# A two-layer graph attention network on one core: another order of work for the last four superchunks of a layer, and one cast moved in the prologue

## The chip, the cores and the metric

The kernel runs on one core of one Trainium2 chip. The core has engines with queues of their own that run side by side: PE multiplies matrices (its weight loads are listed as PEld), DVE and ACT do elementwise work, POOL issues the gathers here (indirect DMAs), and SP issues the other transfers. Each engine takes its own instructions strictly in program order, and waits for the others by semaphores. The metric is the device time of one execution in microseconds (us); lower is better.

## The reference, cut to what matters

There are N = 6250 nodes with 256 features and E = 200000 edges, sorted by destination. The input goes through a layer norm and a ReLU, then through two graph attention layers (4 heads of 64, then 1 head of 256), and is added back at the end.

```python
def _gat(x, src, dst, ea, Wg, a_s, a_d, Wge, a_e, b, n, h, f):
    hx = (x @ Wg).reshape(n, h, f)
    he = (ea @ Wge).reshape(-1, h, f)
    al = leaky_relu(einsum('nhf,hf->nh', hx, a_s)[src] + einsum('nhf,hf->nh', hx, a_d)[dst]
                    + einsum('ehf,hf->eh', he, a_e), 0.2)
    m = segment_max(al, dst, num_segments=n)
    al = exp(al - m[dst])
    al = al / segment_sum(al, dst, num_segments=n)[dst]
    out = segment_sum(hx[src] * al[:, :, None], dst, num_segments=n)
    return out.reshape(n, h * f) + b

te = relu(edge_attr @ We0 + be0) * exp(x @ Wo0 + bo0)[src][:, None]
s2, d2, ea2 = _add_self_loops(src, dst, te, n)      # a loop per node, its features the mean of its edges
x = relu(_gat(x, s2, d2, ea2, Wg0, as0, ad0, Wge0, ae0, bg0, n, HEADS, PH) + x)
te = relu(edge_attr @ We1 + be1) * exp(x @ Wo1 + bo1)[src][:, None]
s2, d2, ea2 = _add_self_loops(src, dst, te, n)
x = _gat(x, s2, d2, ea2, Wg1, as1, ad1, Wge1, ae1, bg1, n, 1, D) + x
return x + orig
```

## The kernel before

**Tiling.** The edges lie in 1563 chunks of 128 (an edge to a partition). A superchunk is 24 chunks (C), and a layer has NS = 66 of them, numbered s = 0 to 65; the last two have 14 and 13 chunks. One pass of the main loop is one superchunk, called a step: k = 0 to 131, layer 0 first (k = 66 is s = 0 of layer 1). The destinations of a superchunk fit into 128 nodes, so its sums are matrix products with one-hot rows S (onehots, L945): each chunk adds S^T G to an accumulator u in PSUM (sums, L1120, two matmuls a chunk). The table T holds a row per node (T[0] of layer 0 is built in the prologue, T[1] of layer 1 is stored by layer 0's steps as their nodes are finished), and G is the rows gathered from it for the edges' sources.

**A step.** With st the step in hand, nx the next, pv the one before and pf the one before that, a step consists of these parts. The names are the functions of the kernel:

- gather(nx), L817: POOL issues an indirect DMA for each chunk of the next step, into one of three G buffers (step k uses buffer k mod 3, so it waits for the sums of step k - 3).
- rphase1(nx), L901 and L906: edge features of the next step, PE into y (one PSUM buffer), ACT into R (one buffer), twice each. load_ea(k + 2), L842, then loads edge features for the step after it (for two steps at a time, one buffer).
- logits(st), L1002 to L1017: DVE; waits for G. ends(st), L1025: PE transposes the scanned maxima into lf.
- spread(nx) and parts(nx), L930, L931, L955 to L960: DVE and one matmul into zad.
- sums(pv): the sums of the step before, on PE.
- links(st), L1035 and L1037 on DVE, then a transpose on PE into lf, L1042.
- blocks(nx), L967, onehots(st), L945 (S has two buffers), finish(pf), L1144 to L1209 in layer 0 and L1149 to L1237 in layer 1: DVE, nodes of the step before last.
- evict(pv) and carry(pv), L1125, L1131, L1133: ACT copies u to U, PE and ACT take out the row that goes on into the next superchunk. carried (L1092 to L1100) adds this row to G of the step in hand, ahead of its sums.
- rows1, rows2, rows3 of pf (L1215 and L1217; L385; L389, L1227): in layer 0 the new table row, by PE, ACT and DVE; rows3 ends with the store to T[1] on SP's queue (L1256). In layer 1 rows3 stores the output: by SP (L1261), or for the last two steps by POOL (L1264, L1265).
- rphase2(nx) and adst(nx), L915 and L974: PE, into zad.
- maxima(st), L1052 to L1079: DVE, waits for the link transpose in lf; ACT makes the exponentials. scale(st), L1110: DVE, multiplies G by them.
- edge_rows(nx), L988 and L991: DVE, waits for adst(nx).

The order of all this is written out by hand. Steps with s = 63 and s = 64, and k = 0, are "at once": their sums, finish, rows, evict and carry run within the step itself. The last step of a layer has a function of its own, last.

**Between the layers.** last issues gather(66), the first of layer 1, with indices (src1) in which nodes of the last two superchunks point at a row of zeros. This gather therefore waits for the T[1] store of s = 63 only; the rows of 64 and 65 are added to G afterwards by matmul (turned_onehots makes the one-hots from a loaded v, L686 and L795; added, L785 and L788). gather(67) waits for the stores of 64 and 65 too, and those wait until gather(66) has landed.

**Prologue.** Tables are built by tiles of x while generators interleave other preparation; indices is one of them: it loads small integer tiles (sc0, bcol, drow, r4, src, dpv) by SP's queue and turns them into floats on DVE (L410 casts dpv to before, L412 casts sc0 to scf).

Of the kernel before, what the change touches and what calls it, by code (L numbers as in the profile page):

```python
# [22 lines left out]
F32 = mybir.dt.float32  # L23
# [8 lines left out]
P = 128  # L32
C = 24
# [45 lines left out]
class Kernel:  # L79
# [311 lines left out]
    def indices(self, wp):  # L391


        nc, cp, a = self.nc, self.cp, self.a
        NS, NCH, N = self.NS, self.NCH, self.N
        V = nc.vector
# [9 lines left out]
        dpv = wp.tile([P, NS], I32, name="dpv", bufs=1)  # L406
        nc.sync.dma_start(dpv, a["dpv"])
        yield
        self.before = cp.tile([P, NS], F32, name="before")
        V.tensor_copy(self.before, dpv)  # L410
# [77 lines left out]
        V.tensor_reduce(self.bad[0:1, 0:1], chk.rearrange("p a b -> p (a b)"), axis=AX.X, op=OP.add)  # L488
        yield
# [81 lines left out]
    def edges(self, ctx):  # L571
        nc = self.nc
# [33 lines left out]
        pv = pf = None  # L606
        ahead, rest = 1, None
        for k, st in enumerate(steps):
            nx = steps[k + 1] if k + 1 < len(steps) else None
# [4 lines left out]
            left = self.groups[ahead][0] - 2 - k if ahead < len(self.groups) else 99  # L614
            if rest is None and left <= 2:
                gi = self.index_load(ahead, self.xp)
                rest = self.index_group(ahead, self.xp, gi)
            if st["s"] + 1 == self.NS:
                self.last(st, pv, nx)
                pv = None  # L620
                continue
# [30 lines left out]
            at_once = k == 0 or self.NS - 3 <= st["s"]  # L652
            if at_once:
                self.sums(st)
# [3 lines left out]
            if rest is not None:  # L658
                for _ in range(7):
                    next(rest, None)  # L660
                if left <= 0:
                    drain(rest)
                    ahead, rest = ahead + 1, None
            pf, pv = pv, st

            if at_once:
                if pf:
                    drain(self.finish(pf))
                    self.rows1(pf)
                    self.rows2(pf)  # L670
                    self.rows3(pf)
                pf = None
                self.evict(st)
                self.carry(st)
            if k == 0 and self.early:
                self.redirect()
        self.flag()

    def last(self, st, pv, nx):

        nc = self.nc
# [5 lines left out]
        if pv and "U" not in pv:  # L687
            self.sums(pv)
            self.evict(pv)
            self.carry(pv)  # L690
        now, half = (C, C) if st["L"].l else (0, C // 2)
        self.onehots(st, 0, now)
        drain(self.logits(st))
        self.ends(st)
        self.onehots(st, now, half)
        self.links(st)
        self.load_fl(st["k"] + 1)
        self.onehots(st, half)
        y = self.rphase1(nx) if nx else iter(())
        next(y, None)  # L700
        next(y, None)
# [3 lines left out]
        drain(y)  # L705
        self.load_ea(st["k"] + 2)
# [6 lines left out]
        if pv:  # L713
            if early:
                w0 = self.turned_onehots(nx, v, 0)
            self.rows1(pv)
            self.rows2(pv)
            self.rows3(pv)
        drain(self.finish(st))
# [394 lines left out]
    def sums(self, st):  # L1114
        nc, L, c = self.nc, st["L"], st["C"]
        G, S = st["G"], st["S"]
        st["u"] = u = self.ps_1.tile([P, 512], F32, name="u")
        for j in range(c):
            i = (j + 1) % c
            nc.tensor.matmul(u[:, :L.W], S[:, i, :], G[:, i, 0:L.W], start=(j == 0), stop=(j == c - 1))  # L1120
# [266 lines left out]
def drain(g):  # L1387
    for _ in g:
        pass
# [93 lines left out]
```

## Time and profile before

| what | us |
|---|---|
| median of 3 runs | 4138.07 (4133.18 to 4142.69) |
| the profiled execution, its time | 4140.48 |
| the profiled execution, its span in the profile | 4138.4 |
| POOL's first gather starts | 97.38 |
| gather(66), the first of layer 1, starts | 2113.58 |
| gather(67) starts | 2153.50 |
| POOL's last gather starts | 4083.89 |
| logits of k = 129, 130, 131 start | 4052.95, 4080.72, 4107.07 |
| scale of k = 129, 130, 131 starts | 4069.70, 4097.16, 4114.03 |
| the last U is evicted from | 4123.60 to 4123.99 |

The profile shows one execution. Its page has the busy time of each engine, the chain of waits that ended last, and the groups of instructions by line. The timeline lists single instructions: start, duration, engine, line, operation, output and inputs, how often, and in square brackets the idle time of the engine before it and what ended that ("[4.88 <-PE lf L1042]": 4.88 us idle, ended by PE's write of lf at L1042). SPq is the issue of a transfer on SP's queue. The clock in the tables of windows is the share of full speed that TensorE was granted.

### The profile page before, as it was taken

Reading aid. Unit: us, or ns where it says so; the run is one execution under the profiler, and the core shown is the slowest. Engines: PE = TensorE matmul, PEld = TensorE weight load, DVE = VectorE, ACT = ScalarE, POOL = GpSimd, SP = SyncE. Lnnn points to the kernel's source line nnn. Section 1 sums busy time; section 2 is a strip of 40 time slices with the busy share of each in tenths; the row PEclk is TensorE's granted clock in tenths of the full one; section 3 lists DMA queues with packets and bytes.
Section 4 is the critical chain, followed back from the end, with each engine's and each line's share of the span. In section 5 each row is a group of like instructions: output and inputs, shape, how many; then the busy total and the mean of one; then the engine's idle time right before and its main releaser. Section 6 shows DMA issues by size and latency. Waiting matters only on the chain.

```text
span 4138.4 us, 34955 instructions
## 1 busy us (share of the span) xinstructions
PE 2815.1 (68%) x10144; PEld 1863.5 (45%) x10144; DVE 2872.6 (69%) x6572; ACT 545.2 (13%) x1256; POOL 2988.4 (72%) x3158
## 2 busy tenths in 40 slices
PE   7577777777676776777676666656566666756665
PEld 5344444444454444544454444434344444434344
DVE  7587777777877778778766666666666666666665
ACT  5111111111111111111111010100101010010100
POOL 2777777777777777777647777777777777777773
PEclk9677877778787787777877777878777777777777
DMA  6545555555554555555435455445545554554552
GB/s 203 155 135 153 149 142 147 147 146 143 154 149 137 154 147 141 149 149 149 125 102 151 132 143 141 137 137 144 141 133 141 141 137 137 145 141 133 141 139 61
DMA packets 246794, 584.74 MB, mean 141 GB/s; under 512 B 63161, under 2 KB 103639, under 8 KB 246529
## 3 DMA queue, kind: packets, MB, share of 16 engines
q0 software_dynamic: 150144, 422.82, 38.7%
q1 hardware_dynamic: 96035, 158.96, 12.3%
q8 instruction: 81, 1.33, 0.1%
q14 instruction: 118, 0.97, 0.1%
q10 hardware_dynamic: 416, 0.67, 0.1%
HBM read 547.98 MB, written 34.34 MB: 141 GB/s over the span
## 4 chain that ended last, share of the span: by engine, by line
POOL 35%; PE 27%; DVE 19%; issue 14%; DMA 2%; ACT 2%; DVEq 0%; ACTq 0%; SPq 0%; POOLq 0%
POOL G L817 35%; PE u L1120 21%; DVE G L1110 9%; PE y L901 3%; DVE lb L930 1%; DMA G<-T,src 1%; PE fin L1131 1%; DVE rt L988 1%; ACT R L906 1%; PE fin L1215 1%; DVE G L1099 1%; ACT carry L1133 1%; DVE G L1079 0%; DVE t1row L389 0%; DVE crow L1095 0%
## 5 line engine op out<-in xcount | busy, mean ns | idle before, releaser
L817 POOL DMA_INDIRECT G<-T,src x3114 | 2970.0, 954 | 1092.2 <-issue 996.5
L1120 PE MATMUL u<-G,S 128*128 128x270 f32 (+1 forms) x6252 | 1714.1, 442 | 34.9 <-DVE G L1110 34.9
L1120 PEld LDWEIGHTS u<-G,S 128*128 128x128 f32 x6252 | 1370.1, 222 | 386.8 <-issue 41.1
L1110 DVE TENSOR_TENSOR G<-G,kps 128x6144 f32<-128x6144 f32 (+2 forms) x140 | 853.3, 6100 | 0.0
L901 PE MATMUL y<-ea,webd 64*128 64x384 f32 (+1 forms) x1056 | 512.4, 615 | 457.4 <-ACT R L906 455.3
L901 PEld LDWEIGHTS y<-ea,webd 64*128 64x128 f32 x1056 | 214.3, 224 | 677.8 <-ACT R L906 535.7
L945 DVE TENSOR_TENSOR S<-kps,loc 128x3072 f32<-128x3072 f32 (+2 forms) x133 | 436.4, 3281 | 0.0
L1025 PE MATMUL lf<-ident,fb 128*36 128x128 f32 (+1 forms) x132 | 54.0, 409 | 533.8 <-DVE fb L1017 306.3
L1025 PEld LDWEIGHTS lf<-ident,fb 128*36 128x36 f32 (+1 forms) x132 | 15.8, 119 | 651.6 <-DVE fb L1017 363.3
L906 ACT ACTIVATE R<-y,webd 128x768 f32<-128x768 f32 x260 | 231.9, 892 | 566.4 <-PE y L901 566.2
L1056 DVE SCALAR_TENSOR_TENSOR m<-fpen,lf,m 128x24 f32<-128x24 bf16 (+1 forms) x66 | 16.5, 250 | 378.9 <-PE lf L1042 378.6
L1002 DVE TENSOR_TENSOR G<-rt,G 128x96 f32<-128x96 f32 (+1 forms) x132 | 30.2, 229 | 262.8 <-DMA G<-T,src 256.7
L915 PE MATMUL zad<-R,wea 128*64 128x384 f32 (+1 forms) x1056 | 205.4, 510 | 0.3 <-DVE aq L967 0.3
L1059 DVE TENSOR_TENSOR mt<-fpen,lf 128x96 f32<-128x96 bf16 (+1 forms) x66 | 16.7, 253 | 253.8 <-PE lf L1042 253.8
L1125 ACT ACTIVATE U<-u 128x270 f32<-128x270 f32 (+1 forms) x132 | 51.8, 392 | 815.8 <-PE u L1120 815.8
L960 PE MATMUL zad<-a,Q 128*128 128x12 bf16 (+1 forms) x132 | 23.7, 179 | 169.3 <-DVE a L958 169.3
L1158 ACT ACTIVATE mw<-mw,mg 128x2 f32<-128x2 f32 x66 | 19.7, 298 | 885.7 <-DVE mg L1157 885.7
L988 DVE STREAM_TRANSPOSE rt<-zad 128x768 f32<-128x768 f32 (+1 forms) x130 | 124.4, 957 | 11.6 <-PE zad L974 11.6
L930 DVE TENSOR_TENSOR lb<-lb,kps 128x1536 bf16<-128x1536 bf16 (+1 forms) x68 | 113.0, 1662 | 12.8 <-DMA lb<-locrow 12.8
L915 PEld LDWEIGHTS zad<-R,wea 128*64 128x64 f32 x1056 | 66.2, 139 | 92.5 <-issue 58.8
L1131 PE MATMUL fin<-U,lsel 128*1 128x270 f32 (+1 forms) x260 | 79.1, 385 | 41.5 <-ACT U L1125 22.5
L1035 DVE TENSOR_TENSOR_SCAN cl<-fl,cl,lf 4x129 f32<-4x129 f32 (+1 forms) x130 | 60.7, 467 | 56.3 <-PE zad L960 52.9
(213 smaller groups left out, 2269.9 us busy)
## 6 DMA issues: line engine op xcount, KB each, us to landing
G<-T,src POOLq DMA_INDIRECT x3114, 2.8
ea<-in_ea_dram SPq DMA_DIRECT2D x64, 768.0 KB
lb<-locrow SPq DMA_DIRECT2D x64, 384.0 KB
T<-t1row SPq DMA_DIRECT2D x66, 260.0 KB
tw<-T SPq DMA_DIRECT2D x66, 258.0 KB
tw<-T SPq DMA_DIRECT2D x66, 134.0 KB
tw<-in_x_dram SPq DMA_DIRECT2D x66, 128.0 KB
out_dram<-fb SPq DMA_DIRECT2D x64, 128.0 KB
```

What stands on the lines that cost most here:

```text
L817: nc.gpsimd.indirect_dma_start(out=G[:, c, 0:L.TW], out_offset=None, in_=self.rows[L.l][0:n * (1 + L.l), :], in_offset=bass.IndirectOffset ...
L901: nc.tensor.matmul(y[:, o], self.webd[l][r, :], ea[r, w], start=True, stop=True)
L906: nc.scalar.activation(R[:, i, :32 * c].rearrange("p (b n) -> p b n", b=2), y.rearrange("p (b n) -> p b n", b=2)[:, :, :16 * c], AF.Relu, ...
L915: nc.tensor.matmul(st["zad"][i * PH:(i + 1) * PH, o], self.wea[l][0], R[:, i, w], start=True, stop=False)
L930: V.tensor_tensor(lb[:, :, :n], lb[:, :, :n], self.k_part.unsqueeze(2).to_broadcast([P, i, n]), op=OP.is_equal)
L945: nc.vector.tensor_tensor(st["S"][:, c0:c1, :], self.k_iota.unsqueeze(1).to_broadcast(w), self.loc[:, o + c0:o + c1].unsqueeze(2).to_broad ...
L988: V.transpose(rv[:, :32 * c].rearrange("p (b n) -> p b n", b=2), z.rearrange("p (b n) -> p b n", b=2)[:, :, :16 * c])
L1025: self.nc.tensor.transpose(self.lf[0:e.shape[1], 1:P + 1], e, self.ident)
L1035: V.tensor_tensor_scan(cl[:H, :], fl[:H, :], lf[:H, 0:P + 1], init, op0=OP.add, op1=OP.max)
L1110: nc.vector.tensor_tensor(v, v, pw[:, c0:c1, :].unsqueeze(3) .to_broadcast([P, c1 - c0, H, L.F]), op=OP.mult)
L1120: nc.tensor.matmul(u[:, :L.W], S[:, i, :], G[:, i, 0:L.W], start=(j == 0), stop=(j == c - 1))
L1131: nc.tensor.matmul(pr[0:1, :L.W], self.lsel[:, s:s + 1], U[:, :L.W], start=True, stop=True)
```

## The change

The last four superchunks of a layer get an order of their own. tight = NS - 4 = 62, so steps s = 62, 63 and 64 run the new function tight, and s = 65 runs last. Sums of a superchunk come in pieces: pieces gives (12, 16) for 24 chunks and (7, 10) for 14. The first piece (0 to 12) stands at the end of the superchunk's own step; in the next step, meet issues ends, then chunks 12 to 16, then the link transpose, then the rest. Step 61 ("enter") keeps the common order but issues its own first piece at its end, the one-hots of 62 and the finish of 60. In the steps of tight, rphase1(nx), load_ea, rphase2(nx) and adst(nx) stand behind maxima, evict, carry and rows2; onehots(nx) are made one step ahead; finish stands at the step's end, except in s = 64 ("final"), where rows3 of 62 and finish of 63 precede maxima and rows 1 to 3 of 63 follow it. In last, rphase1 of layer 1's first step stands behind the rows of 64. In addition the first step of layer 1 (k = 66) has its sums, evict and carry at its end, as k = 0 has. In the prologue the cast of dpv moves from the front of indices to its end.

```diff
@@ -406,8 +406,6 @@
         dpv = wp.tile([P, NS], I32, name="dpv", bufs=1)
         nc.sync.dma_start(dpv, a["dpv"])
         yield
-        self.before = cp.tile([P, NS], F32, name="before")
-        V.tensor_copy(self.before, dpv)
         scf = wp.tile([P, 11, NS], F32, name="scf", bufs=1)
         V.tensor_copy(scf, sc0)
         V.memset(scf[:, 0, 0:1], 0.0)
@@ -486,6 +484,9 @@
             V.tensor_scalar(chk[:, 4, :self.direct], base[0:1, :self.direct], float(N - P), None, op0=OP.is_gt)
         V.memset(self.bad[:, 0:1], 0.0)
         V.tensor_reduce(self.bad[0:1, 0:1], chk.rearrange("p a b -> p (a b)"), axis=AX.X, op=OP.add)
+        yield
+        self.before = cp.tile([P, NS], F32, name="before")
+        V.tensor_copy(self.before, dpv)
         yield
 
     def index_tiles(self):
@@ -603,21 +604,28 @@
         self.adst(steps[0])
         self.edge_rows(steps[0])
 
-        pv = pf = None
-        ahead, rest = 1, None
+        pv = pf = pr = None
+
+        tight = max(self.NS - 4, 1)
+        self.ahead, self.rest = 1, None
         for k, st in enumerate(steps):
             nx = steps[k + 1] if k + 1 < len(steps) else None
             for q in steps[k + 1:k + 3]:
                 if q["L"] is st["L"] and "tw" not in q:
                     self.nodes(q)
             self.load_lb(k + 2)
-            left = self.groups[ahead][0] - 2 - k if ahead < len(self.groups) else 99
-            if rest is None and left <= 2:
-                gi = self.index_load(ahead, self.xp)
-                rest = self.index_group(ahead, self.xp, gi)
+            left = self.groups[self.ahead][0] - 2 - k if self.ahead < len(self.groups) else 99
+            if self.rest is None and left <= 2:
+                gi = self.index_load(self.ahead, self.xp)
+                self.rest = self.index_group(self.ahead, self.xp, gi)
             if st["s"] + 1 == self.NS:
                 self.last(st, pv, nx)
-                pv = None
+                pv = pf = pr = None
+                continue
+            if st["s"] >= tight:
+                self.tight(st, pv, pr, nx)
+                self.index_on(left)
+                pr, pv = pv, st
                 continue
             self.gather(nx)
             drain(self.rphase1(nx))
@@ -649,32 +657,96 @@
                 self.onehots(st)
             drain(self.scale(st))
             self.carried(st)
-            at_once = k == 0 or self.NS - 3 <= st["s"]
-            if at_once:
+            enter = st["s"] + 1 == tight
+            if enter:
+                self.sums(st, 0, self.pieces(st)[0])
+            elif st["s"] == 0:
                 self.sums(st)
             if pf:
                 self.rows3(pf)
             self.edge_rows(nx)
-            if rest is not None:
-                for _ in range(7):
-                    next(rest, None)
-                if left <= 0:
-                    drain(rest)
-                    ahead, rest = ahead + 1, None
-            pf, pv = pv, st
-
-            if at_once:
-                if pf:
-                    drain(self.finish(pf))
-                    self.rows1(pf)
-                    self.rows2(pf)
-                    self.rows3(pf)
-                pf = None
+            if enter:
+                self.onehots(nx)
+                if pv:
+                    drain(self.finish(pv))
+                pr = pv
+            elif st["s"] == 0:
                 self.evict(st)
                 self.carry(st)
+            self.index_on(left)
+            pf, pv = pv, st
             if k == 0 and self.early:
                 self.redirect()
         self.flag()
+
+    def index_on(self, left):
+        if self.rest is not None:
+            for _ in range(7):
+                next(self.rest, None)
+            if left <= 0:
+                drain(self.rest)
+                self.ahead, self.rest = self.ahead + 1, None
+
+    def pieces(self, st):
+
+        c = st["C"]
+        return (c + 1) // 2, c - c // 3
+
+    def meet(self, st, pv, nx):
+
+        p1, p2 = self.pieces(pv) if pv else (0, 0)
+        drain(self.logits(st))
+        self.ends(st)
+        if nx:
+            self.spread(nx)
+            self.parts(nx)
+        if pv:
+            self.sums(pv, p1, p2)
+        self.links(st)
+        if pv:
+            self.sums(pv, p2)
+        self.load_fl(st["k"] + 1)
+
+    def tight(self, st, pv, pr, nx):
+
+
+        final = nx["s"] + 1 == self.NS
+        self.gather(nx)
+        self.meet(st, pv, nx)
+        self.blocks(nx)
+        if final:
+            self.evict(pv)
+            self.carry(pv)
+            if pr:
+                self.rows1(pr)
+                self.rows2(pr)
+                self.rows3(pr)
+            drain(self.finish(pv))
+            drain(self.maxima(st))
+            self.rows1(pv)
+            self.rows2(pv)
+        else:
+            drain(self.maxima(st))
+            self.evict(pv)
+            self.carry(pv)
+            if pr:
+                self.rows1(pr)
+                self.rows2(pr)
+        drain(self.rphase1(nx))
+        self.load_ea(st["k"] + 2)
+        self.rphase2(nx)
+        self.adst(nx)
+        if final:
+            self.rows3(pv)
+        drain(self.scale(st))
+        self.carried(st)
+        self.sums(st, 0, self.pieces(st)[0])
+        if pr and not final:
+            self.rows3(pr)
+        self.edge_rows(nx)
+        self.onehots(nx)
+        if not final:
+            drain(self.finish(pv))
 
     def last(self, st, pv, nx):
 
@@ -684,26 +756,15 @@
             self.gather(nx, 0, self.src1)
             v = self.gp[(nx["k"] + 1) % 3].tile([P, C * 270], F32, name="v", tag="G").bitcast(BF)
             nc.sync.dma_start(v[:, :early * P], self.srow.partition_broadcast(P))
-        if pv and "U" not in pv:
-            self.sums(pv)
-            self.evict(pv)
-            self.carry(pv)
-        now, half = (C, C) if st["L"].l else (0, C // 2)
-        self.onehots(st, 0, now)
-        drain(self.logits(st))
-        self.ends(st)
-        self.onehots(st, now, half)
-        self.links(st)
-        self.load_fl(st["k"] + 1)
-        self.onehots(st, half)
-        y = self.rphase1(nx) if nx else iter(())
-        next(y, None)
-        next(y, None)
+        if not pv:
+            self.onehots(st)
+        self.meet(st, pv, None)
         if nx:
             nc.vector.tensor_scalar(self.src, self.src, 2.0, None, op0=OP.mult)
         drain(self.maxima(st))
-        drain(y)
-        self.load_ea(st["k"] + 2)
+        if pv:
+            self.evict(pv)
+            self.carry(pv)
         drain(self.scale(st, 3))
         self.carried(st)
         self.sums(st)
@@ -716,6 +777,9 @@
             self.rows1(pv)
             self.rows2(pv)
             self.rows3(pv)
+        if nx:
+            drain(self.rphase1(nx))
+            self.load_ea(st["k"] + 2)
         drain(self.finish(st))
         if early:
             w1 = self.turned_onehots(nx, v, 1)
@@ -1111,13 +1175,14 @@
                                     .to_broadcast([P, c1 - c0, H, L.F]), op=OP.mult)
             yield
 
-    def sums(self, st):
+    def sums(self, st, a=0, b=C):
         nc, L, c = self.nc, st["L"], st["C"]
         G, S = st["G"], st["S"]
-        st["u"] = u = self.ps_1.tile([P, 512], F32, name="u")
-        for j in range(c):
+        if a == 0:
+            st["u"] = self.ps_1.tile([P, 512], F32, name="u")
+        for j in range(a, min(b, c)):
             i = (j + 1) % c
-            nc.tensor.matmul(u[:, :L.W], S[:, i, :], G[:, i, 0:L.W], start=(j == 0), stop=(j == c - 1))
+            nc.tensor.matmul(st["u"][:, :L.W], S[:, i, :], G[:, i, 0:L.W], start=(j == 0), stop=(j == c - 1))
 
     def evict(self, st):
         L = st["L"]
```

## The prediction

> **What bounds the kernel now.** I read the page first: the engine line, the chain that ended last, the groups.
>
> ```profile
> PE 2815.1 (68%) x10144; PEld 1863.5 (45%) x10144; DVE 2872.6 (69%) x6572; ACT 545.2 (13%) x1256; POOL 2988.4 (72%) x3158
> ...
> POOL 35%; PE 27%; DVE 19%; issue 14%; DMA 2%; ACT 2%; DVEq 0%; ACTq 0%; SPq 0%; POOLq 0%
> ...
> L817 POOL DMA_INDIRECT G<-T,src x3114 | 2970.0, 954 | 1092.2 <-issue 996.5
> ...
> L1002 DVE TENSOR_TENSOR G<-rt,G 128x96 f32<-128x96 f32 (+1 forms) x132 | 30.2, 229 | 262.8 <-DMA G<-T,src 256.7
> ```
>
> No engine is over 72% busy, but POOL's gathers need 0.954 + 0.30 us of issue each: 24 x 1.25 = 30.0 us per superchunk (step), and DVE's first instruction of a step waits 256.7 us in all for them. A step's own work is worth nothing while POOL runs without a gap. So I looked next for POOL's gaps in the timeline. Beside some fifteen of 0.5 to 1.35 us in layer 0, they are: its start at 97.38, and the end of layer 0. After 2153.5 there is none to the last gather (4083.89 + 0.95). What moves POOL's start or the layer boundary moves the end by as much; otherwise only what follows the last gathers counts.
>
> The timeline of the prologue (DVE), of the boundary, and of the tail of layer 1:
>
> ```profile
> 41.12 0.20 DVE L410 CAST before<-dpv 128x66 f32<-128x66 int32 x1 [7.41 <-DMA dpv<-in_dpv_dram]
> ```
>
> ```profile
> 2046.07 13.98 PE L1120 MATMUL u<-G,S 128*128 128x270 f32 x48
> ...
> 2059.99 0.25 PE L1042 MATMUL lf<-ident,cl 36*128 36x36 f32 x1
> ...
> 2060.27 0.26 DVE L1059 TENSOR_TENSOR mt<-fpen,lf 128x96 f32<-128x96 bf16 x1 [4.88 <-PE lf L1042]
> 2060.33 0.94 POOL L817 DMA_INDIRECT G<-T,src  x1 [8.69 <-PE lf L1042]
> ...
> 2110.67 0.34 SPq L1256 DMA_DIRECT2D T<-t1row  x1
> ...
> 2113.58 0.94 POOL L817 DMA_INDIRECT G<-T,src  x1 [37.31 <-DMA T<-t1row]
> ...
> 2153.50 0.94 POOL L817 DMA_INDIRECT G<-T,src  x1 [7.21 <-DVE G L788]
> ```
>
> ```profile
> 4052.95 0.20 DVE L1002 TENSOR_TENSOR G<-rt,G 128x24 f32<-128x24 f32 x1 [5.70 <-DMA G<-T,src]
> ...
> 4067.93 0.25 PE L1042 MATMUL lf<-ident,cl 33*128 33x33 f32 x1
> ...
> 4068.22 0.25 DVE L1056 SCALAR_TENSOR_TENSOR m<-fpen,lf,m 128x24 f32<-128x24 bf16 x1 [5.41 <-PE lf L1042]
> ...
> 4076.30 12.28 PE L1120 MATMUL u<-G,S 128*128 128x261 f32 x48 [6.01 <-DVE G L1110]
> ...
> 4101.09 9.12 PE L1120 MATMUL u<-G,S 128*128 128x261 f32 x28 [5.07 <-DVE G L1110]
> ...
> 4115.03 8.54 PE L1120 MATMUL u<-G,S 128*128 128x261 f32 x26 [2.27 <-DVE G L1110]
> ...
> 4123.60 0.39 ACT L1125 ACTIVATE U<-u 128x261 f32<-128x261 f32 x1 [4.08 <-PE u L1120]
> ```
>
> The reader is to see: DVE stands still 7.41 us for one small load; POOL stands still 37.3 us until the table row of s=63 is stored; and in the tail the link transpose L1042 sits on PE behind a whole superchunk's sums (12 to 14 us), so maxima, scale and the next sums come one after another. The last U ends at 4123.99 and the span 14.4 us later.
>
> **The change, part by part.**
>
> *The cast.* The instruction that follows it (scf) needs a load whose packets were through by about 31.6 us, so DVE goes on 7.4 us earlier. From 40 to 80 us DVE is busy 37.2 of 40 us, and PE (8.7 us) and ACT (10.3 us) idle at the same place, so the chain to the T stores (93.4) and POOL's start (97.38) moves with it; the x tiles of that stretch land at 45.5 and are wanted at 53.65 - 7.4 = 46.2 at the earliest. The cast itself (0.20 us) is done later, long landed. -7.4; -4 if a later load or PE takes half of it back, -8 at best. POOL's start carries it to the end.
>
> *Layer 0's last steps.* I walked the new order of each engine with the old rows' durations (sums 0.56 us per chunk of two matmuls; 13.98/24 = 0.58 and 12.28/24 = 0.51 are the rows; scale 6.46, finish 4.93, onehots 3.26, y 1.55 and R 0.90 twice, zad 1.51). Removed: the link transpose waits for 4 chunks of sums in place of 24, and the sums of 63 and 64 no longer stand whole inside their steps. Added: a wait. rphase1(nx) now stands behind links, the rest of the sums, evict, carry and rows2, so zad(63) is ready at 2041.9, where DVE's scale, carried and table row end at 2037.1. DVE stands 4.8 us at edge_rows(63); queued behind it on DVE are onehots(63), finish(61) and logits(63). logits(63) starts at 2051.9 against 2042.58: 9.3 late. But its maxima then wait 4 chunks, not 24: 2058.1 against 2060.27. At s=63 DVE waits again for adst, 2.7 us, and logits(64) start at 2081.6 against 2086.03. The final step puts evict(63), rows3(62) and finish(63) ahead of maxima(64): 2101.1 against 2094.0. Its payment is that rows of 63 need no sums at their end: rows3(63)'s exponent comes on ACT behind R(65), and the store can be issued at 2108.8 against 2110.67. That is -1.9 if nothing is ahead of it on SP's queue. But load_ea(66) is: it waits for y(65), 2107.6 in my walk, where it went out at 2090.57. Of this transfer's 2.9 us I charge 2.4 to the store, so gather(66) starts at 2114.1: +0.5. At 0.50 us per chunk and no queueing the store is 2.2 us earlier still (about -3); at 0.65 and a full ea transfer ahead, +4. Both go into the range. The gather of s=65 starts 3.6 us later than at 2060.33, with POOL idle from then to 2113. The stores of 64 and 65 (exponent of 65 at 2142.6, before 2142.87) still precede the landing of gather(66), which frees them, so the step to 2153.5 moves as gather(66) does.
>
> [...]
>
> *Layer 1's first step.* Its sums, evict and carry come at its end now; maxima of the next come some 0.8 us later, under POOL's pace with its 30.0 us steps: 0. If that cover were gone it would cost the 0.8.
>
> *Tail of layer 1.* logits(129) is set by gather(129) landing, 4052.95 in both. From there, with the old rows' durations:
> - maxima(129) after ends, 4 chunks and links: 4058.2, was 4068.22 (-10.0).
> - scale(129) ends 4066.2; the evict chain, y, R, zad and adst of 130 are through at 4068.8; edge_rows, onehots and finish(128): logits(130) start 4074.6, was 4080.72 (-6.1; the wait for adst and onehots and finish in front take 3.9 back).
> - rest of sums(129): 4084.3, evict and finish(129): 4087.9; maxima and scale(130): 4093.4, was 4101.04 (-7.6).
> - edge_rows, onehots: logits(131) 4096.6, was 4107.07 (-10.5); maxima wait only 3 chunks; scale(131) starts 4101.7, was 4114.03 (-12.3).
> - sums(131), 13 chunks: 4110.8; last U ends 4111.2, was 4123.99: **-12.8**. The 14.4 us behind it stay.
>
> The new waits here: DVE's edge_rows for adst, with onehots and the next logits queued behind. The path has some 48 chunks' worth of PE: at 0.50 us a chunk it would be -15.4, at 0.65 (9.12/14, 8.54/13) -8.3. The span between these rows is the clock:
>
> ```profile
> 2048.00:2050.00 2.00, 2.00 (x6) 1.53 (x5) 2.00 (x1) 0.00 (x0) 1.51 (x2) 0.50 0.39 99
> ...
> 2055.00:2059.00 4.00, 4.00 (x20) 3.31 (x19) 0.39 (x2) 0.00 (x0) 0.00 (x0) 1.00 0.00 0
> ```
>
> Columns: window, its length, busy time (instructions) of PE, PEld, DVE, ACT, POOL, then granted clock. At 0.50 a matmul takes 0.33 us, at 1.00 0.20, PE equally busy; the sums of before were mixtures, so I take 0.56. [...] With every piece at 0.67 us a chunk the tail would be -12.8 + 48 x 0.11 = -7.5.
>
> **Sum**: -7.4 + 0.5 + 0 - 12.8 = -19.7 on a span of 4138.4, so 4118.7; the profiled execution took 4140.48 with what lies around it, and the median of the runs is 4138.07, which gives **4118.4**. Corner to corner: -26.4 to -8.3.
>
> **The rivals.**
> 1. *The prologue gives nothing.* If another load, or PE, sets the same chain, scf only waits elsewhere. For: the chain of waits leads through dpv alone because it came last. Against: scf's load was through 9 us earlier and DVE is 93% busy afterwards. 4138.1 - 12.3 = 4125.8; with the boundary at +4, 4129.3. Chance 0.12.
> 2. *Cold pieces.* Tail -8.3, boundary +4, prologue -4 to -7.4: 4126.4 to 4129.8, and a little beyond if the prologue is lost too (4133.8). For: the 14- and 13-chunk rows at 0.65. Against: the 24-chunk rows at 0.51 to 0.58. Chance 0.15.
> 3. *Slower.* The one mechanism: edge_rows(nx) waits for adst, which hangs on the chain sums, evict, carry, rows2, y, R, zad through PE and ACT, in each of s=62, 63, 64 of layer 0; if the pieces win nothing back, the 9.3 us by which logits(63) are late come at every step, and with the 2.4 us of the ea load that hangs on the same y the store of s=63 is 3 x 9.3 + 2.4 = 30.3 us late: 4138.1 - 20.2 + 30.3 = 4148.2. It decides from 20.2 + 8.3 = 28.5 us. For: that wait is new and real. Against: lateness of logits is paid back in the same step by 20 chunks that are no longer ahead of the transpose. Chance 0.07.
>
> **How the numbers follow.** 0.2%, 8.3 us, is about what a measurement can tell from none. The forecast has 0.66: faster. Rival 1 is faster in nearly all of it; rival 2 is split, two thirds of it above 4129.8. Faster 0.80, same 0.13, slower 0.07. Range 4109 to 4131: the corners and the few us by which runs differ (4133.18 to 4142.69).
>
> **What will show it.** POOL's first gather near 90.0; gather(66) at about 2106.7 (2114.1 - 7.4) and the store of s=63 right behind an ea load; DVE idle before L988 at the last steps of layer 0, 3 to 5 us each; POOL without a gap after; from gather(129)'s landing to the last U's end 58.3 us in place of 71.04; sums in runs of 12, 4 and 8 chunks. It is wrong if POOL starts at 97 still, if gather(66) comes over 8 us later than POOL's start moved, or if the tail's span is over 63 us.

## The result and the profile after

The changed kernel takes 4120.34 us (median of 7 runs, 4109.04 to 4125.54), the kernel before 4133.18 us in the runs beside it (4129.35 to 4143.16). The ratio is 0.9959 with a 95% interval of 0.9942 to 0.9976: 10 to 24 us faster, most likely 17. The profiled execution took 4109.04 us, its span 4107.1, and was the fastest of the seven.

The page of the changed kernel, the lines that answer to those of before:

```profile
PE 2807.1 (68%) x10144; PEld 1848.2 (45%) x10144; DVE 2872.1 (70%) x6571; ACT 545.5 (13%) x1256; POOL 2988.5 (73%) x3158
...
POOL 38%; PE 24%; DVE 18%; issue 15%; DMA 2%; ACT 2%; DVEq 0%; SPq 0%; ACTq 0%; POOLq 0%
...
L881 POOL DMA_INDIRECT G<-T,src x3114 | 2970.2, 954 | 1075.2 <-issue 995.8
```

No engine does less. In this execution POOL's share of the chain is 38% and PE's 24% (before 35% and 27%); in a second execution of the changed kernel (below) they are 34% and 28%, so the shares say nothing of the change. Where the time went is read from marks of the timeline (us):

| stretch | before | after | forecast of the step |
|---|---|---|---|
| start to POOL's first gather | 97.38 | 89.62 (-7.8) | -7.4 |
| first gather to the end of gather(64) | 1954.25 | 1941.82 (-12.4) | 0 |
| end of gather(64) to gather(66), "the boundary" | 61.95 | 65.90 (+4.0) | +0.5 |
| gather(66) to gather(67) | 39.92 | 39.99 | 0 |
| gather(67) to POOL's last gather | 1930.39 | 1929.66 (-0.7) | 0 |
| last gather to the end, "the tail" | 54.51 | 40.11 (-14.4) | -12.8 |

The two spans differ by 31.3 us, the medians by 12.8. The second row is the reason: of its steps only the last ones, from the end of 61 on, were changed, and the same changed kernel in another execution took 1952.09 there (below). Without it the terms come to -18.9, near the ratio's 17.

The prologue of the changed kernel in the timeline:

```profile
33.78 0.52 DVE L410 CAST scf<-sc 128x726 f32<-128x726 int32 x1
...
89.62 0.95 POOL L881 DMA_INDIRECT G<-T,src  x1 [67.08 <-issue]
```

The cast to scf starts at 33.78 without a wait (before: 41.23, behind 7.41 us of idle), and the gain reaches POOL's start whole.

The boundary, lines in order of time. L1052 is edge_rows, the first L1185 the second piece of a superchunk's sums (4 chunks), L1106 the link transpose; the gathers of POOL are the first of gather(65), gather(66) and gather(67):

```profile
2019.79 0.98 DVE L1052 STREAM_TRANSPOSE rt<-zad 128x768 f32<-128x768 f32 x1 [4.35 <-PE zad L1038]
...
2033.29 3.95 PE L1185 MATMUL u<-G,S 128*128 128x270 f32 x8
...
2037.17 0.32 PE L1106 MATMUL lf<-ident,cl 36*128 36x36 f32 x1
...
2042.53 0.94 POOL L881 DMA_INDIRECT G<-T,src  x1 [11.09 <-PE u L1185]
...
2051.63 0.65 DVE L1052 STREAM_TRANSPOSE rt<-zad 128x448 f32<-128x448 f32 x1 [4.01 <-PE zad L1038]
...
2077.05 0.43 DVE L389 TENSOR_TENSOR t1row<-fin,bias 128x260 f32<-128x260 f32 x1 [11.40 <-PE fin L385]
...
2090.85 0.40 SPq L906 DMA_DIRECT2D ea<-in_ea_dram  x1
2091.82 0.33 SPq L1321 DMA_DIRECT2D T<-t1row  x1
...
2097.34 0.98 POOL L881 DMA_INDIRECT G<-T,src  x1 [38.81 <-DVE al L1072]
...
2137.33 0.94 POOL L881 DMA_INDIRECT G<-T,src  x1 [7.17 <-DVE G L852]
```

DVE's new wait is there, 4.35 and 4.01 us (and 1.73 in the final step). A longer one, 11.40 us, stands in the final step: DVE waits for the table row of 62, whose matmuls stand on PE behind the rest of the sums of 63, evict and carry. The store of s=63 goes out right behind the load of edge features, and gather(66) follows it after 5.52 us; it was 2.91. The releaser that the page names for gather(66), a DVE instruction, is an inference; the packets in the trace fit the store: those of the load run from 2091.90 to 2095.47, those of the store, issued at 2091.82, from 2095.00 to 2096.12.

The pieces' clock, columns as in the prediction:

```profile
2033.30:2037.00 3.70, 3.70 (x9) 2.48 (x9) 1.05 (x4) 0.00 (x0) 0.00 (x0) 0.50 0.01 2
2037.50:2042.00 4.50, 4.50 (x16) 3.52 (x16) 4.13 (x10) 0.26 (x1) 0.00 (x0) 0.80 0.00 0
2038.50:2039.50 1.00, 1.00 (x4) 0.80 (x3) 0.85 (x5) 0.21 (x1) 0.00 (x0) 0.59 0.00 0
```

4 chunks took 3.95 us, 0.99 a chunk, at half clock; the 8 chunks after them 4.83, 0.60 a chunk, since the clock rose to 1.00 only around 2039.3.

The tail of layer 1:

```profile
4039.63 3.64 PE L1185 MATMUL u<-G,S 128*128 128x261 f32 x8
...
4043.48 0.25 DVE L1120 SCALAR_TENSOR_TENSOR m<-fpen,lf,m 128x24 f32<-128x24 bf16 x1 [2.87 <-PE lf L1106]
...
4058.80 0.18 DVE L1066 TENSOR_TENSOR G<-rt,G 128x14 f32<-128x14 f32 x1
...
4085.78 5.99 PE L1185 MATMUL u<-G,S 128*128 128x261 f32 x26
...
4091.81 0.39 ACT L1190 ACTIVATE U<-u 128x261 f32<-128x261 f32 x1 [2.23 <-PE u L1185]
```

From logits(129), 4036.91, to the last U's end, 4092.20, there are 55.3 us (forecast 58.3, before 71.0).

### The profile page after: what moved, and what is told of

Read it like the earlier page. It is cut to its first block, busy times and chain, and to the rows that moved or that the text cites. A ratio compares the mean times of both kernels' runs of the same rounds, so it can differ in the third digit from the quotient of the medians.

```text
span 4107.1 us, 34953 instructions
## 1 busy us (share of the span) xinstructions
PE 2807.1 (68%) x10144; PEld 1848.2 (45%) x10144; DVE 2872.1 (70%) x6571; ACT 545.5 (13%) x1256; POOL 2988.5 (73%) x3158
## 4 chain that ended last, share of the span: by engine, by line
POOL 38%; PE 24%; DVE 18%; issue 15%; DMA 2%; ACT 2%; DVEq 0%; SPq 0%; ACTq 0%; POOLq 0%
POOL G L881 38%; PE u L1185 19%; DVE G L1174 8%; PE y L965 2%; DMA G<-T,src 1%; DVE lb L994 1%; PE fin L1196 1%; DVE rt L1052 1%; ACT R L970 1%; PE fin L1280 1%; ACT carry L1198 1%; DVE G L1163 1%; DVE S L1009 0%; DVE t1row L389 0%; DVE G L1143 0%
## 5 line engine op out<-in xcount | busy, mean ns | idle before, releaser
L1185 PE MATMUL u<-G,S 128*128 128x270 f32 (+1 forms) x6252 | 1700.2, 438 | 26.3 <-DVE G L1174 26.3
L1185 PEld LDWEIGHTS u<-G,S 128*128 128x128 f32 x6252 | 1354.5, 219 | 370.6 <-issue 37.8
L1009 DVE TENSOR_TENSOR S<-kps,loc 128x3072 f32<-128x3072 f32 x132 | 436.1, 3304 | 0.0
L1066 DVE TENSOR_TENSOR G<-rt,G 128x96 f32<-128x96 f32 (+1 forms) x132 | 30.1, 228 | 255.4 <-DMA G<-T,src 249.8
L1052 DVE STREAM_TRANSPOSE rt<-zad 128x768 f32<-128x768 f32 (+1 forms) x130 | 124.5, 958 | 26.7 <-PE zad L1038 26.7
```

The source lines that it names most:

```text
L1009: nc.vector.tensor_tensor(st["S"][:, c0:c1, :], self.k_iota.unsqueeze(1).to_broadcast(w), self.loc[:, o + c0:o + c1].unsqueeze(2).to_broad ...
L1052: V.transpose(rv[:, :32 * c].rearrange("p (b n) -> p b n", b=2), z.rearrange("p (b n) -> p b n", b=2)[:, :, :16 * c])
L1185: nc.tensor.matmul(st["u"][:, :L.W], S[:, i, :], G[:, i, 0:L.W], start=(j == 0), stop=(j == c - 1))
```

## The experiments

All runs are read by the same marks. The twelve runs fell on two kinds of chips, and this decides how each can be used. On one kind the kernel before took 4141 us and POOL set the pace, as in the case's own profiles. On the other it took 4921 to 4923 us. The sums on PE, first on the slow kind (moved cast alone, second run), then on the other (changed kernel, second run); columns as in the page's fifth part:

```profile
L1121 PE MATMUL u<-G,S 128*128 128x270 f32 (+1 forms) x6252 | 1889.8, 460 | 639.9 <-issue 600.6 <-DVE G L1111 27.3 <-DMA G<-T,src 9.5
```

```profile
L1185 PE MATMUL u<-G,S 128*128 128x270 f32 (+1 forms) x6252 | 1704.2, 439 | 26.0 <-DVE G L1174 26.0
```

On the slow kind PE stands 600.6 us before its sums without waiting for anything that the profile shows; a step takes some 35 to 37 us and POOL waits some 5 to 8 us in each for a buffer. I call it a chip where PE is held up, though PE is not alone: in the first run of the moved cast DVE stands 31.7 us in all at edge_rows, and ACT 2.86 us before one R, with nothing but their own issue named as what ended it, where in the whole profile of the kernel before all such waits of DVE come to 4 us and those of ACT to 2. POOL's ahead of its gathers are the same on both kinds (975.9 and 995.2 us in the two profiles above). The mean granted clock is lower there too, 0.73 against 0.78; whether that is a cause or goes along with the waits was not tried, nor was anything else about the reason. There a shift of POOL's start or of the boundary need not reach the end, so only the marks and the ratios to the kernel before on the same chip are used.

| run | chip | boundary | gather(66) to (67) | tail | ratio (95%) |
|---|---|---|---|---|---|
| changed, again | POOL paces | 68.87 | 39.98 | 40.83 | 0.9967 (0.9952 to 0.9982) |
| whole sums | POOL paces | 58.15 | 40.24 | 37.85 | 0.9924 (0.9901 to 0.9947) |
| keep warm | POOL paces | 75.01 | 44.84 | 61.72 | 1.0026 (1.0010 to 1.0043) |
| y early, layer 0 | POOL paces | 53.52 | 39.79 | 41.08 | 0.9930 (0.9908 to 0.9951) |
| moved cast alone | PE held up | 66.68, 66.86 | 44.74, 46.18 | 56.34, 56.34 | 0.9989 (0.9980 to 0.9998), 0.9991 (0.9982 to 1.0001) |
| layer 0 as before | PE held up | 66.39, 67.08 | 47.44, 43.99 | 49.70, 49.59 | 0.9985 (0.9976 to 0.9994), 0.9985 (0.9975 to 0.9994) |
| later load | PE held up | 69.63 | 49.12 | 50.29 | 1.0019 (1.0011 to 1.0028) |
| y early, both layers | PE held up | 60.31 | 54.69 | 54.26 | 1.0035 (1.0022 to 1.0048) |
| whole, reordered | PE held up | 62.01, 61.06 | 58.08, 56.06 | 47.34, 47.66 | 0.9964 (0.9952 to 0.9976), 0.9966 (0.9952 to 0.9979) |

**The changed kernel again.**

> The changed kernel unaltered, run on the same chip as the three below, for its trace there. If POOL sets the pace as in the case's two profiles: first gather 89.6, boundary (end of gather(64) to start of gather(66)) 64 to 67, gather(66) to gather(67) 40.0, tail (POOL's last gather to the end) 39 to 42, time 0.995 to 0.997 of the kernel before. If PE is held up by its own issue, as in the runs of the prologue and of the order of layer 0: boundary 70 to 72, tail about 50, ratio 0.999 to 1.003.

POOL paced. First gather 89.57, tail 40.83, ratio as foretold; the boundary, 68.87, is 2 over. First gather to the end of gather(64) took 1952.09 us, as long as the kernel before in its profile (1954.25): some 10 of the 12.4 us of the table above belong to that execution and not to the change. The chain of waits is that of before too (POOL 34%, PE 28%, DVE 19%). The boundaries of this one kernel differ by 3 us between two executions (65.90 and 68.87); differences under that say nothing.

**The moved cast alone.** Only the two hunks of the prologue.

```diff
         yield
-        self.before = cp.tile([P, NS], F32, name="before")
-        V.tensor_copy(self.before, dpv)
         scf = wp.tile([P, 11, NS], F32, name="scf", bufs=1)
...
+        yield
+        self.before = cp.tile([P, NS], F32, name="before")
+        V.tensor_copy(self.before, dpv)
         yield
```

> The kernel before with the moved cast alone. Marks read from the trace: POOL's first gather (before 97.4, changed kernel 89.6); the boundary, from the moment POOL runs out of gathers after gather(64) to the start of gather(66) (before 61.9, changed 65.9); the tail, from the start of POOL's last gather to the end of the span (before 54.5, changed 40.1). Theory (DVE's wait for dpv set the whole prologue): first gather at 89.6 within 1, boundary 61.9 and tail 54.5 within 3, time 7.8 us under the kernel before, ratio 0.998. Rival (the shift in the changed kernel came with a warmer PE in that execution): first gather at 95 to 97, ratio 1.000.

> The kernel before with the moved cast alone, a second time, for a chip on which POOL paces. Theory: first gather 89.6 within 1 (before 97.4), boundary 60 to 64, tail 53 to 56, ratio 0.998 with an interval of about 0.0015. Rival (POOL's earlier start is lost again in the first steps): first gather 89.6, but ratio 0.9995 or more.

Both runs fell on chips where PE is held up: first gather at 91.89 and 91.36, below the rival's 95 to 97 (no profile of the kernel before was taken there), ratios 0.9989 and 0.9991, some 5 us. That is a gain smaller than 7.8, where POOL's start is not what the end hangs on, and the second run's interval reaches 1.0001. The boundary, 66.7 and 66.9, is longer on this kind of chip without any change to it. On a chip where POOL paces it was not run alone; there its worth in time was not measured, and the term rests on the first gather of five profiles with the moved cast (88.84 to 90.02, before 97.38).

**Layer 0 in the order of before**, prologue and layer 1 as changed. last0 is the function last of the kernel before.

```diff
-            if st["s"] >= tight:
+            late = st["L"].l == 0 and self.NS - 3 <= st["s"]
+            if st["s"] >= tight and st["L"].l:
...
-                self.last(st, pv, nx)
+                (self.last if st["L"].l else self.last0)(st, pv, nx)
```

> The changed kernel with the order of before in the last steps of layer 0; layer 1's steps and the prologue stay changed. Theory (the new order costs 4 us at the end of layer 0 and earns 14 in layer 1): first gather 89.6, boundary back from 65.9 to 62 within 2, tail 40 within 2, time 4 us under the changed kernel, 20 to 22 under the kernel before, ratio 0.995. Rival (the 4 us are chance of the clock's phase): boundary 65 to 67 as in the changed kernel, and no difference between the two in time.

> The changed kernel with the order of before in the last steps of layer 0, a second time, for a chip on which POOL paces. Theory (the new order loses 3 to 6 us at the boundary and wins 14 in layer 1's tail): first gather 89.6, boundary 61 to 64 in place of 65.9 and 68.9, tail 40 to 41, time 3 to 6 us under the changed kernel, ratio 0.994 to 0.996. Rival (the boundary differs between executions by as much as between the two orders): boundary 65 to 69.

On both chips the boundary is that of the old order (66.4 and 67.1, as with the moved cast alone: 66.7, 66.9), against 69.63 with the new one and the later load: with the new order it is 2.5 to 3 us longer even without the load ahead of the store, at the edge of what two executions differ by. The tail, 49.6, is 6.7 under the old order's 56.34 on these chips, not 14, and in time this kernel (0.9985) can't be told from the moved cast alone (0.9989 and 0.9991). On the first of the two chips the kernel with the new order in layer 0 and the later load stands at 1.0019, 15 us above this one: there the new order of layer 0 is a loss. That the time would lie 4 us under the changed kernel's was not tested, since no run of that kernel fell on such a chip.

**The load of edge features behind the store.**

```diff
         drain(self.rphase1(nx))
-        self.load_ea(st["k"] + 2)
+        if not final:
+            self.load_ea(st["k"] + 2)
...
         if final:
             self.rows3(pv)
+            self.load_ea(st["k"] + 2)
```

> The changed kernel, the load of edge features for layer 1's first two steps issued behind the T[1] store of s=63 in the final step. Theory (the store's packets stand behind that load on SP's queue): from the issue of the store to gather(66) 2.9 us in place of 5.5, boundary 63.3 in place of 65.9, nothing else. Rival (the store lands late for another reason, or is issued late alone): 5 to 5.5 us as in the changed kernel.

PE was held up, but this mark does not depend on that: store at 2544.01, gather(66) at 2546.97, 2.96 us, against 5.52 and 5.43 in the two profiles of the changed kernel. The store is now issued ahead of the load (2544.01 and 2544.44), where in the changed kernel's profile it is issued behind it and its packets start as the load's end (2095.00 and 2095.47). The queueing is shown; 2.5 us of the boundary are the load. The time, 1.0019, is slower than the kernel before on this chip, with an interval clear of 1; of all runs on such chips this kernel is nearest to the changed one, which was not run there itself.

**y at the front of the new steps**, in both layers, then in layer 0 alone.

```diff
         self.gather(nx)
+        drain(self.rphase1(nx))
+        self.load_ea(st["k"] + 2)
         self.meet(st, pv, nx)
...
-        drain(self.rphase1(nx))
-        self.load_ea(st["k"] + 2)
         self.rphase2(nx)
```

> The changed kernel with rphase1(nx) and load_ea back at the front of the new steps, as in the common step; everything else as changed. Theory (DVE's new wait at edge_rows for the chain evict, rows, y, R, zad is on the path of the boundary): DVE's waits before L1052 in s=62, 63, 64 of layer 0 (4.35, 4.01, 1.73 us) under 1 us each, the T[1] store of s=63 no longer behind the load, boundary 53 to 57 in place of 65.9, tail 1 us shorter. Rival (what the wait costs is paid back anyway by the wait for the link transpose): boundary 63, by the load alone.

> The changed kernel with rphase1(nx) and load_ea at the front of the new steps in layer 0 alone. Theory (the boundary lost by DVE's wait at edge_rows and by the load ahead of the T[1] store): boundary 10 us under the changed kernel's on this chip, the store to gather(66) 2.9 us, tail as the changed kernel's; of the 10, gather(67) keeps 5 to 10, since it waits for the stores of 64 and 65; time 5 to 10 us under the changed kernel. Rival (the stores of 64 and 65 take all of it back): gather(66) to gather(67) longer by as much as the boundary is shorter, time unchanged.

The first, with PE held up, has no wait of DVE at edge_rows any more. It took 9.3 us off the boundary of the run beside it (69.63 to 60.31), and gather(67) gave 5.6 of them back; its tail was 4 us longer and it was the slowest of its four. The second ran where POOL paces, beside the changed kernel: boundary 53.52 against 68.87, 15.4 us, and gather(67) kept all of it. The timeline of the second:

```profile
2056.48 0.63 DVE L1057 STREAM_TRANSPOSE rt<-zad 128x448 f32<-128x448 f32 x1
...
2092.58 0.34 SPq L1326 DMA_DIRECT2D T<-t1row  x1
2095.46 0.94 POOL L886 DMA_INDIRECT G<-T,src  x1 [27.81 <-DMA T<-t1row]
```

DVE does not wait at edge_rows, and the gather follows the store by 2.88 us, here with the store named as its releaser. Of the 15.4 us (10 were expected), 2.5 are the load (5.43 to 2.88); the other 12.8 are an earlier store. DVE's waits at the two edge_rows ahead of it (7.07 and 2.20 us in the changed kernel beside it) are gone, and the exponent of the new table row no longer stands on ACT behind R of the next step: there the row was ready at 2100.28 and the exponent began at 2104.78, 4.5 us later, here the store follows the row at once. Smaller waits take about 1 us of this back. The ratio, 0.9930 against 0.9967, is 15 us, give or take some 11 by the two intervals, and neither gather(66) to gather(67) nor the tail moved by more than 0.3: the whole term reaches the end.

**Sums not cut.**

```diff
-        return (c + 1) // 2, c - c // 3
+        return c, c
```

> The changed kernel, its sums not cut: all chunks of a superchunk stand where its first piece stood, at the end of its own step. Theory (what pays is the place of the link transpose ahead of nothing but started sums, and the cut in three costs restarts of PE): the T[1] store of s=63 comes 10 to 12 us earlier than in the changed kernel, boundary 53 to 57 where POOL paces, tail within 2 us of the changed kernel's. Rival (the cut is what keeps the transposes early; whole sums push ends and links back by up to 10 us): boundary 66 or more, tail 3 to 8 us longer.

The rival falls, and the direction of the theory holds: the store of s=63 comes 10.8 us earlier against the end of gather(64), the boundary is 58.15, 10.7 less but above the range, the tail 37.85, 3.0 less where 2 were the limit, and the time 4107.29 us against 4124.89. The marks hold 13.7 of these 17.6 us. The timeline of the boundary (the sums of 63, then in step 64 the link transpose, DVE's wait for the table row of 62 and the first maxima):

```profile
2056.76 11.48 PE L1185 MATMUL u<-G,S 128*128 128x270 f32 x48
...
2070.86 0.25 PE L1106 MATMUL lf<-ident,cl 36*128 36x36 f32 x1 [0.64 <-DVE cl L1101]
2075.86 0.43 DVE L389 TENSOR_TENSOR t1row<-fin,bias 128x260 f32<-128x260 f32 x1 [4.82 <-PE fin L385]
...
2081.19 0.21 DVE L1123 TENSOR_TENSOR mt<-fpen,lf 128x56 f32<-128x56 bf16 x1
```

24 chunks in one run took 11.48 us, 0.48 a chunk, in a window at a clock of 0.97; cut in three they took 5.65 + 3.95 + 4.14 = 13.7 in the changed kernel beside it. The whole sums end before the next logits do, so the transpose waits for DVE alone, where in the cut version it waits for the second piece. The cut thus costs 2.2 us of PE's time in this superchunk, which does not make the 10.7 by itself. Ahead of the store DVE no longer waits for the link transposes of 62 and 63 (3.10 and 2.84 us in the changed kernel beside it), its wait for the table row of 62 falls from 11.42 to 4.82, and its two waits at edge_rows grow by 2.7 (7.42 and 4.59, were 7.07 and 2.20): 9.8 in all. How much of that is the place of the pieces behind the next logits, and how much their clock, was not separated.

**Keeping PE warm.** 24 matmuls whose product is not read.

```diff
+        self.keep_warm(24)
         self.edge_rows(nx)
...
+    def keep_warm(self, n):
+        y = self.ps_y.tile([P, 1024], F32, name="y")
+        for _ in range(n):
+            self.nc.tensor.matmul(y[:, 0:256], self.ident, self.wg[0][:, 0, 0:256], start=True, stop=True)
```

> The changed kernel with 24 unread matmuls of 128x256 behind the first piece of each new step, to keep PE busy until the next ends (about 5 us of work at full clock); they compute nothing that is used. In the changed kernel's profile the second piece, 4 chunks, took 3.95 us at a clock of 0.50 after 5.5 to 6.6 us of idle PE. Theory (the idle time before it sets that clock): the second piece takes 1.6 to 2.2 us at a clock near 1.0, each step's maxima come 1.8 us earlier, boundary 2 to 4 us shorter, tail 1 to 3 us shorter. Rival (the clock drops by a time of its own, whatever PE does): second pieces of 3 to 4 us as before in most of the six places, boundary and tail the same within 1 us or longer by the added work.

```profile
2048.09 2.07 PE L1192 MATMUL u<-G,S 128*128 128x270 f32 x8
...
4054.73 10.52 PE L756 MATMUL y<-wg,ident 128*128 128x256 f32 x48
4065.09 0.27 PE L1096 MATMUL lf<-ident,fb 128*33 128x128 f32 x1
```

```profile
2048.10:2050.10 2.00, 2.00 (x12) 1.42 (x9) 1.26 (x4) 0.00 (x0) 0.00 (x0) 1.00 0.01 1
```

The second piece took 2.07 us at a clock of 1.00 where it had taken 3.72 to 3.95 at 0.50 to 0.55: with the idle time ahead of it filled, the clock of this piece was not low. But the added work took 10.5 us where I had reckoned 5, and the next ends stood behind it on PE: boundary 6 us and tail 21 us longer, 1.0026. For these pieces the part of the idle time in the clock is shown, its price in time is not.

**Whole sums, reordered.** In the new steps evict and carry stand ahead of maxima and y, zad and adst ahead of rows1; the final step of layer 0 has finish(63) and its store ahead of y and of the load.

```diff
         self.blocks(nx)
+        self.evict(pv)
+        self.carry(pv)
+        drain(self.maxima(st))
+        if ahead:
...
+            drain(self.finish(pv))
+            self.rows1(pv)
+            self.rows2(pv)
+            self.rows3(pv)
+        drain(self.rphase1(nx))
+        self.load_ea(st["k"] + 2)
```

> The kernel with whole sums, and in the new steps: evict and carry ahead of maxima, rphase1, rphase2 and adst ahead of rows1 and rows2; in the final step of layer 0 rows3(62), finish(63) and the T[1] store of s=63 ahead of rphase1 and of the load of edge features; in the final step of layer 1 finish(129) and its store behind the one-hots. Theory (what is left at the boundary is DVE's wait for adst and the load ahead of the store): where POOL paces, boundary 48 to 53 (whole sums alone 58.3, changed kernel 65.9 and 68.9), gather(66) to gather(67) 40 to 43, tail 35 to 37.5 (whole sums alone 37.9), time 5 to 9 us under whole sums alone, ratio to the kernel before 0.990 to 0.992. Rival (the stores of 64 and 65 hold gather(67), so nothing is left to gain): gather(66) to gather(67) 46 or more, time as whole sums alone, 0.992 to 0.993.

> The reordered kernel with whole sums a second time, for a chip on which POOL paces. Theory there: boundary 50 to 55 and gather(66) to gather(67) 40 to 44 (their sum 93 to 97; whole sums alone 98.5, changed kernel 105.9 and 108.9, before 101.9), tail 35 to 37.5, ratio to the kernel before 0.990 to 0.992. Rival (as on the chip where PE is held up by its issue, the stores of 64 and 65 hold gather(67)): gather(66) to gather(67) 48 or more, the sum of the two 99 or more, ratio 0.992 to 0.994. If PE is held up here too: ratio 0.996 again.

Both runs fell on chips where PE is held up. There it is the fastest kernel of all, 0.9964 and 0.9966, with the shortest tail, 47.3 and 47.7; the rival is right about the boundary: gather(66) to gather(67) takes 58.1 and 56.1, so what the store of 63 gains is given back to those of 64 and 65. Boundary and that step take 120.1 and 117.1 us together, more than with the moved cast alone (111.4 and 113.0); 9 us of the gain lie in the tail. Whether it beats whole sums alone where POOL paces stays open.

## Why the prediction was right, and where its steps were off

The time, 4120.34 us, lies 2 us from the forecast and in its range, and the direction was right; the ratio's 17 us stand against 19.7. That it is only 2 us is partly luck: the kernel before took 4133.18 us beside it, 4.9 less than the median that the forecast started from. The chip was luck as well: all the forecast's rows come from a chip where POOL paces, and nothing in it foresaw the other kind. The steps, as they were put:

1. **The cast: -7.4, whole to POOL's start.** -7.8 in the profile. Rival 1 is out where POOL paces, as far as POOL's start goes.
2. **Boundary: +0.5.** It was +4.0, and +6.9 in the second execution, so this is the term that was mis-sized. The store's queueing was right: the 2.4 us charged were an estimate from the load's 2.9 us, which no run shows as such; from the store's issue to gather(66) it took 5.52 and 5.43 us with the load ahead, 2.91 before and 2.96 with the load behind, so 2.5 to 2.6. A row of the kernel before points the same way: the loaded v, issued at 2111.35 behind the store, has its first packet at 2112.36, when the store's last packet ends (2112.34). Also nearly right were the two waits at edge_rows (7.5 us foretold; 8.4, or 9.3 in the second execution). Two things were off. The second pieces were charged 0.56 us a chunk and took 0.93 to 0.99: 1.5 to 1.7 us more ahead of each link transpose. In the final step PE also made y (1.75 twice) and the new table row (2.10) at a granted clock of 0.50, where the kernel before took 0.97, 1.52 and 1.15. This step alone, from logits(64) to the store, took 30.1 us in both executions, 27.2 in the forecast. The store of s=63 was thereby issued 1.3 and 4.4 us later against the end of gather(64) than before (60.38 and 63.44, was 59.04), in place of 1.9 earlier.
3. **What the new wait costs.** The prediction let it stand as paid back. Without it and the load, layer 0's new order would have had a boundary of 53.5, 8 us better than before: the wait is the largest cost inside the change that a run took out, some 13 us with y's place, hidden in a sum that comes out near nothing. The place of the pieces, some 10 us in the run of whole sums, is the next. Rival 3 had the mechanism and its place; its price, 30.3 us over before, was not reached.
4. **Layer 1's first step: 0.** gather(67) to the last gather: -0.7.
5. **Tail: -12.8.** -14.4 and -13.7. The second piece of 128 was slower here too (3.64 us), and maxima(129) come 6.6 us after logits(129) start where 5.3 was foretold; but the 12 chunks of 129 that were left took 5.8 us, not 6.7, and the last sums, 13 chunks, 5.99 us, 0.46 a chunk, not 7.3. Rival 2, cold pieces, was right for the second pieces behind 3.3 to 6.6 us of idle PE (3.64 to 3.95 us), not for the others: that of 129, behind 1.76 us, took 2.01.

The terms add up in each execution: -18.9 us without the second row in the first, and -13.6 in the second, whose ratio, 0.9967, gives 13.7.

In layer 0 of the changed kernel the second pieces, behind 5.4 to 6.6 us of idle PE, ran at a clock of 0.50 to 0.55 for their 3.7 to 3.95 us, and at 1.00, in 2.07 us, when that idle time was filled. The full clock came back some 3.4 to 6 us after such a piece had started, PE being busy nearly all the time: in the rows above, 0.50 from 2033.30 on, 0.59 between 2038.5 and 2039.5. The 3.4 is worked out from the mean of 0.55 over the 3.7 us from 2048.50 in the second execution. The kernel before had shown the like: PE was busy with a superchunk's sums from 2046.07, behind idle times of 5.80, 1.15 and 1.11 us, and the clock stayed 0.50 until about 2051.8 (0.74 between 2051.5 and 2052.0, 1.00 between 2051.8 and 2052.5), 5.7 us. At the prediction's 0.33 us a matmul for that clock, 4 chunks take 2.7 us, so it could have foreseen them at 0.50 throughout; it charged them the 0.56 us a chunk of whole sums and kept a cold price of 0.67 for the range. Even that lies under the 0.93 to 0.99 measured, and what the rest is stays open. What else sets the clock was not shown.

The prediction's reading of one profiled execution was safe only for marks: the stretch of layer 0 ahead of the boundary moved by 10 us between two executions of one kernel.

## What to carry to other kernels

When a long product stands ahead of a short one that the next stage waits for, first ask whether it can start early enough to be done in time. Pieces that are left for later stand behind the next stage's own work and may start at a low clock (0.50 to 0.55 in layer 0); here the whole sums were the better by 18 us. When a producer is moved back behind a chain on other engines, look for who stands in order behind its consumer: the wait at edge_rows and the new place of y cost 13 us in a place that looked like slack. A store that an idle engine waits for should not share its queue with a bulk load issued just ahead of it, which here cost 2.5 us.

## What the runs showed of the hardware that was not expected

The same kernel took 4133 to 4141 us on some chips and 4921 to 4923 on others. The difference shows above all as waits of PE for its own issue, 600.6 us ahead of the sums' matmuls and 143.4 ahead of y's, where the other kind shows none; the sums' matmuls also took 1889.8 us in place of 1704.2. POOL's gathers took 0.95 us each on both, and on the slow kind POOL waited some 5 to 8 us a step for a buffer. Why the engines are held up was not found. What a change is worth differs with it: the new order of layer 1 shortened the tail by 14 us where POOL paces and by 6.7 where PE is held up, and the new order of layer 0 with the later load was slower there than the order of before. Whether the changed kernel gains anything on such a chip was not measured.
